# First stage of a convolution block: one reader of PSUM, squares from SBUF, padded copies two groups ahead, stores on SyncE

## The chip, the core and the metric

The kernel runs on one core of a Trainium2 chip. A core has a matrix engine (PE in the profile, with PEld for its weight loads), VectorE (DVE), ScalarE (ACT), GpSimd (POOL) and SyncE (SP), each with its own instruction queue, an on-chip memory SBUF, a smaller memory PSUM, divided into banks, into which PE writes, and DMA engines that move data to and from DRAM. An engine works through its instructions in order and waits on semaphores for what the others have to deliver. The metric is the time of one launch on the device, in microseconds (us).

## The reference

The input x has 32 images of 384 channels of 28 x 28 points, all in float32. Layer 0 is a convolution block, layer 1 a gate on its result.

```python
# layer 0
y = conv_general_dilated(x, dw_w, padding=3, feature_group_count=C)  # 7x7, each channel by itself
y = transpose(y + dw_b, (0, 2, 3, 1))
mu = mean(y, -1);  var = mean(square(y - mu), -1)
y = (y - mu) * rsqrt(var + 1e-6) * ln_g + ln_b
y = gelu(einsum('bhwc,cf->bhwf', y, w1) + b1)          # 384 -> 1536
gx = sqrt(sum(square(y), (1, 2)))
y = grn_g * (y * gx / (mean(gx, -1) + 1e-6)) + grn_b + y
x = x + transpose(einsum('bhwf,fc->bhwc', y, w2) + b2)  # 1536 -> 384
# layer 1
avg, mx, mn = mean, max, min of x over the points
logits = concat([avg @ W1.T, grouped(mx, W2_1) * W2_2, mn @ W3.T]) @ Wfc.T
return sigmoid(logits + x)
```

The part that matters here is the first: the depthwise convolution, and the mean and variance over the 384 channels, for which the kernel sums the convolved values and their squares.

## The kernel before, in words

The program has two stages. The second (from L897 on) goes image by image through the two large products, with a scheme that saves multiplications: sums and differences ("forms") of the weights and of the activations go into fewer matmuls. The first stage, the block `with ExitStack() as one`, does the depthwise convolution of all images and prepares the weight forms. The change lies in the first stage alone.

**The convolution.** The loop `for s in range(NK)` has 48 steps of 8 channels (TC). A step is four pairs of channels; `conv` handles one pair. Its input is `xt`, in which the rows of the padded image stand on the partitions and (block of rows, image) on the 224 columns. For each channel three matmuls (L696, L698, L700) multiply a band matrix of the filter (`tmat`) with `xt` into one half of a PSUM bank `pc` (pool psc, 4 banks). The bank is then read three times: DVE turns it by 32 x 32 blocks into `yt` (L703), DVE adds it to the sum `acc` (L711), and ACT squares each of the two channels into `sq` (L717, pool sqp, two tiles of half a step each). After every second pair POOL adds `sq` to `ssum` (L723). At the end of the step POOL's queue stores `yt` to `yd` in DRAM (L870). `yt` has two buffers (pool ycp). Since `keep` keeps the program order on an engine, the order in the code is the order in the queue.

**Making xt.** Four steps share one `xt`, which is made one `xt` ahead. The images come in 8 groups of 4. For each group `load_x` (SP) brings 32 channels from DRAM, 8 groups ahead. `pad_x` copies them into one of three padded tiles `xpad` (L477, on ACT; L475 on POOL for the first groups). `turn_x` then has PE turn the tile 128 x 128 at a time into a PSUM tile `pt` (L487, pool psx, 3 tiles): four blocks for h = 0, which DVE copies to `xt` (L496), and three for h = 1, which ACT copies (L498). `spread` places two groups into each step, between the pairs, and calls `pad_next(i + 1)`, so that a pad runs one group ahead of its turning.

**Loads and forms.** At the top of a step SP issues `load_t` (L424), the band matrices of three steps later. Some steps bring weights as well (`later`): before such a load a POOL copy (L816) from `acc` writes one column of its target, which holds the load back to this step. In steps 7 to 11 PE centres the first weights (`center_w`). In steps 12 to 20 and 24 to 44 `form_w` makes the weight forms u1 and u2 in three buffers (`ufp`), with an ACT or POOL instruction to start (L562, L559) and POOL additions (L565). They are stored to u1d and u2d at the end of the next step, on POOL's queue (L886).

**The end.** Steps 46 and 47 run as two halves of the images (`pc_half`), so that stage 2 can begin with the first. `finish`, once for each half, turns sums into the mean and 1/sqrt(var + eps): an add, a reduce of the four rows of `ssum` (L748), some small instructions (L754 to L757), the root on ACT (L758), a reciprocal (L759), a turn (L760) and the store to `rsd` (L761), from which stage 2 reads it back. `sq`, `ssum` and `acc` are indexed by unturned points throughout; only the result is turned.

Of the kernel before, what the change touches and what calls it, by code (L numbers as in the profile page):

```python
# [8 lines left out]
F32 = mybir.dt.float32  # L9
AF = mybir.ActivationFunctionType  # L10
# [3 lines left out]
P = 128  # L14
# [183 lines left out]
def convnext_gate_kernel(  # L198
# [163 lines left out]
    with ExitStack() as one:  # L362
# [76 lines left out]
        NG = B // NB  # L439
        NXI = 8  # L440
        xi_last = tp.tile([P, NT], F32, name="xi_last")
        ssum = finp.tile([P, SQ, N], F32, name="ssum")
        acc = finp.tile([P, 2, N], F32, name="acc")
        dws = finp.tile([P, 1], F32, name="dws")
        lr = tp.tile([P, CB, 2], F32, name="lr")
# [33 lines left out]
        def turn_x(i, h, xt, eng=nc.vector):  # L479

            g = i % NG
            xv = xt.rearrange("p c (j b) -> p j c b", j=NJ)
            j0, j1 = 4 * h, min(NJ, 4 * h + 4)
            pt = psx.tile([P, 4, P], F32, tag="pt", name=f"pt_{i}_{h}")
            for j in range(j0, j1):
                keep(
                    nc.tensor.transpose(  # L487
                        pt[:, j - j0, :],
                        xpad[i % NPAD][:, j * RW : (j + 1) * RW, :].rearrange("p r w -> p (r w)"),
                        ident,  # L490
                    )
                )
            dst = xv[:, j0:j1, :, g * NB : (g + 1) * NB]
            src = pt[:, : j1 - j0, :].rearrange("p j (c q) -> p j c q", q=NB)
            if eng is nc.vector:
                keep(eng.tensor_copy(dst, src))  # L496
            else:
                keep(eng.activation(dst, src, AF.Identity))  # L498

        def new_xt(k):  # L500
            return xtp.tile([P, XC, N], F32, tag="xt", name=f"xt_{k}")
# [114 lines left out]
        def pad_next(i):  # L616
            if i < GT:
                pad_x(i)
                if i + AHEAD < GT:
                    load_x(i + AHEAD)  # L620
# [7 lines left out]
        for i in range(NG):  # L628
# [15 lines left out]
            for h in range(2):  # L644
                turn_x(i, h, xt, (nc.vector, nc.scalar)[h])
        pad_next(NG)

        later = {
            **{
# [22 lines left out]
        def conv(s, c2, yt, xt, b0, b1):  # L672

            t = tmat[s % NT2]
            nb = b1 - b0
            if not nb:
                return
            if nb == B:
                pc = psc.tile([P, 2, 256], F32, tag="pc", name=f"pc_{s}_{c2}_{b0}")
            else:  # L680

                pc = pcs.pop(0)
                pcs.append(pc)
            for ci in range(2):
                c = 2 * c2 + ci
                if nb == B:
                    po = pc[:, ci, :N]
                    xc = xt[:, s % SK * TC + c, :]
                    after, before = xc[:, B:], xc[:, : N - B]
                    lo, hi = po[:REACH, : N - B], po[:, B:]  # L690
                else:
                    po = pc[:, ci, :N].rearrange("p (j b) -> p j b", b=B)[:, :, b0:b1]
                    xc = xt[:, s % SK * TC + c, :].rearrange("p (j b) -> p j b", b=B)[:, :, b0:b1]
                    after, before = xc[:, 1:], xc[:, : NJ - 1]
                    lo, hi = po[:REACH, : NJ - 1], po[:, 1:]
                keep(nc.tensor.matmul(po, t[:, c, P : 2 * P], xc, start=True, stop=False))  # L696
                keep(
                    nc.tensor.matmul(lo, t[:, c, 2 * P : T0 + MW], after, start=False, stop=False)  # L698
                )
                keep(nc.tensor.matmul(hi, t[:, c, :P], before, start=False, stop=True))  # L700
            cc = s * TC + 2 * c2
            cy = 2 * c2
            keep(nc.vector.transpose(yt[:, cy : cy + 2, :], pc[:, :, :N]))  # L703

            def part(v):
                if nb == B:
                    return v
                return v.rearrange("p c (j b) -> p c j b", b=B)[:, :, :, b0:b1]

            a = part(acc)  # L710
            keep(nc.vector.tensor_tensor(a, a, part(pc[:, :, :N]), ALU.add))  # L711
            nonlocal sq
            if cy % SQ == 0:
                sq = sqp.tile([P, SQ, N], F32, tag="sq", name=f"sq_{cc}_{b0}")
            for ci in range(2):
                keep(
                    nc.scalar.activation(  # L717
                        part(sq)[:, cy % SQ + ci], part(pc[:, :, :N])[:, ci], AF.Square,
                        bias=dwb[:, cc + ci : cc + ci + 1], scale=1.0,
                    )  # L720
                )
            if cy % SQ == SQ - 2:
                nc.gpsimd.tensor_tensor(part(ssum), part(ssum), part(sq), ALU.add)  # L723

        sq = None

# [2 lines left out]

        pcs = []  # L730

        fins = []

        def finish(half, b0, b1):

            if not half:
                fins.append(sqp.tile([P, SQ, N], F32, tag="sq", name="fin"))
                nc.vector.memset(fins[0][:, 0], 0.0)
            fin = fins[0]

            def part(v):
                return v.rearrange("p (j b) -> p j b", b=B)[:, :, b0:b1]

            rs, s2 = (part(fin[:, i]) for i in range(2))
            mu, va = (part(acc[:, i]) for i in range(2))
            (nc.vector.tensor_tensor(mu, mu, va, ALU.add))
            (
                nc.vector.tensor_reduce(  # L748
                    s2,
                    ssum.rearrange("p c (j b) -> p j b c", b=B)[:, :, b0:b1],  # L750
                    AX.X, ALU.add,
                )
            )
            (nc.vector.tensor_scalar(mu, mu, dws, 1.0 / C, ALU.add, ALU.mult))  # L754
            (nc.vector.tensor_tensor(va, mu, mu, ALU.mult))
            (nc.vector.scalar_tensor_tensor(va, s2, 1.0 / C, va, ALU.mult, ALU.subtract))
            (nc.vector.tensor_scalar(va, va, 0.0, EPS, ALU.max, ALU.add))  # L757
            nc.scalar.activation(s2, va, AF.Sqrt)  # L758
            (nc.vector.reciprocal(rs, s2))  # L759
            (nc.vector.transpose(fin[:, 2], fin[:, 0]))  # L760
            nc.sync.dma_start(rsd[half], fin[:, 2])  # L761

        STEPS_K = SK * PAIRS
        plan = [[] for _ in range(STEPS_K)]
# [3 lines left out]
        def spread(k, q, xn):  # L768
            for n in plan[q]:
                g, h = divmod(n, 2)  # L770
                i = k * NG + g
                if h == 0:
                    pad_next(i + 1)
                turn_x(i, h, xn, (nc.vector, nc.scalar)[h])

        def first_image(part):

# [25 lines left out]
        for s in range(NK):  # L803
# [8 lines left out]
            if s in later:  # L812

                dst, src = later[s]
                first = dst[:, :1] if len(dst.shape) == 2 else dst[:, 0, :1]
                nc.gpsimd.tensor_copy(first, acc[: dst.shape[0], 0, :1])  # L816
                nc.sync.dma_start(dst, src)
            if si == 0:
                xn = new_xt(k + 1) if k + 1 < NX else None
            if s == NK - 2:  # L820
                warm = smp.tile([P, 1], F32, tag="warm", name="warm", bufs=1)
                nc.scalar.activation(warm, eps_t, AF.Sqrt)
            if s == NK - 1:
# [33 lines left out]
            elif s < NK - 2:  # L857
                for c2 in range(PAIRS):
                    conv(s, c2, yt, xt, 0, B)
                    q = (s - U1 + 5) * PAIRS + c2  # L860
                    if 0 <= q < 2 * PAIRS:
                        for n in range(q * 3 // 2, (q + 1) * 3 // 2):
                            center_w(n)
                    elif q in (2 * PAIRS + 2, 2 * PAIRS + 5, 2 * PAIRS + 8):
                        n = FB + 4 * ((q - 2 * PAIRS) // 3)
                        for i in range(4):
                            center_w(n + i)
                    if k + 1 < NX:
                        spread(k + 1, si * PAIRS + c2, xn)
                keep(nc.gpsimd.dma_start(yd[:, s * TC : (s + 1) * TC, :], yt))  # L870
                yt = new_yt(f"yt_{s + 1}")
                if s == 35:
                    yi = yis[0] = yip.tile([P, CB, NQD, YR], F32, tag="yi", name="yi_0")
                    for cb in range(2):
                        load_y_part(0, yi, cb, 0, P)
                if NK - 4 <= s:
                    first_image(s - NK + 4)
                if s == NK - 3:
                    load_y_part(0, yis[0], CB - 1, 0, P - 2 * TC)
            if si == SK - 1:  # L880
                xt = xn
            if s == SG:
                gate_weights()
                nc.vector.tensor_reduce(dws, dwb, AX.X, ALU.add)
            for dst, u in stores:
                keep(nc.gpsimd.dma_start(dst, u))  # L886
            stores.clear()
            for i in range(NS):
                if s != U1 + i * 3 // 5:
                    continue  # L890
# [430 lines left out]
```

## Time and profile before

| | |
|---|---|
| median of 3 runs | 3113.83 us (3113.55 to 3114.8) |
| the profiled execution: its time | 3120.5 us |
| its span | 3118.8 us |
| busy in the span: PE / DVE / ACT / POOL | 97% / 64% / 58% / 80% |
| share of the last chain: PE / POOL / DMA / DVE / ACT | 79% / 7% / 5% / 4% / 2% |

The span runs from the first to the last instruction of one profiled execution. Its busy shares are averages over both stages. In the first stage, up to about 577 us, these groups matter (line, engine, operation, output and inputs, number | busy us, mean ns of one | idle before it, and what ended that):

```profile
L723 POOL TENSOR_TENSOR ssum<-ssum,sq 128x896 f32<-128x896 f32 (+1 forms) x100 | 201.2, 2012 | 142.8 <-ACT sq L717 142.3
L717 ACT ACTIVATE sq<-pc,dwb 128x224 f32<-128x224 f32 x368 | 144.2, 444 | 262.2 <-DVE acc L711 228.0 <-POOL ssum L723 24.2 <-POOL u L565 5.0
L703 DVE STREAM_TRANSPOSE yt<-pc 128x448 f32<-128x448 f32 x184 | 119.0, 647 | 225.3 <-PE pc L700 164.5 <-DMA yd<-yt 59.0 <-PE pt L487 1.6
L711 DVE TENSOR_TENSOR acc<-acc,pc 128x448 f32<-128x448 f32 x184 | 107.1, 582 | 5.5 <-POOL ws L816 5.5
L565 POOL TENSOR_TENSOR u<-u,ws 128x384 f32<-128x384 f32 (+1 forms) x66 | 68.9, 1047 | 3.4 <-ACT u L562 0.5
L477 ACT ACTIVATE xpad<-room 128x784 f32<-128x784 f32 x77 | 66.1, 858 | 0.0
L496 DVE COPY xt<-pt 128x512 f32<-128x512 f32 x96 | 65.2, 679 | 14.8 <-PE pt L487 14.7
L498 ACT ACTIVATE xt<-pt 128x384 f32<-128x384 f32 x96 | 47.0, 490 | 10.8 <-PE pt L487 7.9 <-DMA dwb<-in_cvec 3.0
L559 POOL TENSOR_TENSOR u<-ws 128x384 f32<-128x384 f32 (+1 forms) x26 | 29.1, 1126 | 44.3 <-DMA u2d<-u 27.3 <-DMA u1d<-u 12.2 <-DMA ws<-in_w 4.5
L870 POOL DMA_DIRECT2D yd<-yt x46 | 26.1, 568 | 0.0
```

The first number after the bar is the sum over all instructions of the group, the second the mean of one; the idle time that follows lies just before the instructions of the group on their engine.

### The profile page before, as it was taken

What the parts mean: (1) busy time and instruction counts of PE and PEld (TensorE: products, weight loads), DVE (VectorE), ACT (ScalarE), POOL (GpSimd) and SP (SyncE); (2) the same over time, 40 slices, a digit from 0 to 9 for tenths busy, and PEclk for the clock granted to TensorE, in tenths of its full rate; (3) what the DMA queues carried; (4) which work ended last, traced back from release to release, by engine and by line L of the source; (5) the groups of instructions that cost most, each with busy time, mean ns of one, the idle gap of its engine ahead of it and who ended that gap; (6) DMA issues with size and microseconds to landing.
All of it is one profiled execution on the core that took longest, in us unless ns stands there. A gap on an engine that the chain in (4) does not pass through costs nothing.

```text
span 3118.8 us, 44072 instructions
## 1 busy us (share of the span) xinstructions
PE 3019.9 (97%) x14435; PEld 2441.6 (78%) x14435; DVE 1992.4 (64%) x4555; ACT 1808.0 (58%) x3004; POOL 2484.5 (80%) x1912
## 2 busy tenths in 40 slices
PE   8998889799999999999999999999999999999998
PEld 8988889567777777777777777777777777777777
DVE  5554445666666666666666666666666666666666
ACT  4454445365666666666666666666666666666662
POOL 4466667569888888888888888888888888888897
PEclk9999999899999999999999999999999999999999
DMA  9888877644666666666666666666666666666545
GB/s 348 318 299 318 293 297 286 214 136 157 201 201 201 202 201 201 201 201 201 201 202 201 202 201 201 202 200 202 199 201 201 202 201 201 202 201 201 195 152 201
DMA packets 277900, 674.16 MB, mean 216 GB/s; under 512 B 30863, under 2 KB 98730, under 8 KB 271658
## 3 DMA queue, kind: packets, MB, share of 16 engines
q1 hardware_dynamic: 255364, 579.39, 56.4%
q0 software_dynamic: 9344, 53.61, 4.2%
q10 hardware_dynamic: 12966, 38.34, 3.2%
q8 instruction: 118, 1.93, 0.3%
q14 instruction: 108, 0.88, 0.1%
HBM read 575.57 MB, written 95.68 MB: 215 GB/s over the span
## 4 chain that ended last, share of the span: by engine, by line
PE 79%; POOL 7%; DMA 5%; DVE 4%; issue 2%; ACT 2%; ACTq 0%; DVEq 0%; SPq 0%; POOLq 0%
PE ph_C L974 13%; PE ph_A L974 12%; PE ph_B L974 11%; PE pz_C L1104 7%; PE pz_A L1104 7%; PE pz_D L1104 7%; PE pz_F L1104 7%; PE pc L696 2%; PE pz_H L1104 2%; PE pz_I L1104 2%; PE pz_E L1104 2%; PE pc L700 2%; PE pc L698 2%; POOL d_room L1065 2%; DVE room L315 2%
## 5 line engine op out<-in xcount | busy, mean ns | idle before, releaser
L326 ACT ACTIVATE y<-y,fv,gsc 128x784 f32<-128x784 f32 x372 | 359.1, 1031 | 463.3 <-DVE gsc L1012 463.3
L1065 POOL TENSOR_TENSOR d_room<-y 128x588 f32<-128x588 f32 x253 | 364.3, 1441 | 291.7 <-PE pz_B L1104 195.5
L933 ACT ACTIVATE y<-y,b1f 128x784 f32<-128x784 f32 x384 | 350.3, 945 | 209.8 <-DVE y L991 179.5
L974 PE MATMUL ph_C<-room,ws 128*128 128x392 f32 x1240 | 462.6, 495 | 5.8 <-DVE y L989 3.0
L974 PE MATMUL ph_B<-room,ws 128*128 128x392 f32 x1240 | 460.9, 494 | 4.2 <-DVE room L358 4.2
L974 PE MATMUL ph_A<-room,ws 128*128 128x392 f32 x1240 | 460.0, 493 | 4.0 <-ACT te L981 2.0
L1065 POOL TENSOR_TENSOR d_room<-d_room,y 128x588 f32<-128x588 f32 x308 | 440.8, 1436 | 16.8
L974 PEld LDWEIGHTS ph_C<-room,ws 128*128 128x128 f32 x1240 | 233.3, 190 | 190.1 <-DVE y L989 29.4
L974 PEld LDWEIGHTS ph_A<-room,ws 128*128 128x128 f32 x1240 | 235.7, 190 | 177.5 <-ACT te L981 2.7
L974 PEld LDWEIGHTS ph_B<-room,ws 128*128 128x128 f32 x1240 | 235.7, 191 | 169.4 <-POOL ssum L723 4.3
L946 ACT ACTIVATE junk<-y 128x784 f32<-128x784 f32 x384 | 329.0, 857 | 9.0
L1065 POOL TENSOR_TENSOR d_room<-y,d_room 128x588 f32<-128x588 f32 x214 | 306.1, 1436 | 26.9 <-PE pz_D L1104 15.8
L723 POOL TENSOR_TENSOR ssum<-ssum,sq 128x896 f32<-128x896 f32 (+1 forms) x100 | 201.2, 2012 | 142.8 <-ACT sq L717 142.3
L358 POOL TENSOR_TENSOR room<-room 128x392 f32<-128x392 f32 x303 | 303.5, 1019 | 11.9
L717 ACT ACTIVATE sq<-pc,dwb 128x224 f32<-128x224 f32 x368 | 144.2, 444 | 262.2 <-DVE acc L711 228.0
L1065 POOL TENSOR_TENSOR y<-y 128x588 f32<-128x588 f32 x180 | 258.7, 1437 | 7.1
L703 DVE STREAM_TRANSPOSE yt<-pc 128x448 f32<-128x448 f32 x184 | 119.0, 647 | 225.3 <-PE pc L700 164.5
L987 DVE TENSOR_TENSOR y<-y,ph_B 128x392 f32<-128x392 f32 x256 | 137.4, 557 | 156.0 <-ACT y L933 123.5
L985 DVE TENSOR_TENSOR y<-y,ph_C 128x392 f32<-128x392 f32 x384 | 212.5, 560 | 25.2
L696 PE MATMUL pc<-xt,tmat 128*128 128x224 f32 x736 | 205.9, 362 | 8.9 <-ACT xt L498 8.9
L1104 PE MATMUL pz_A<-d_room,u 128*128 128x196 f32 x1050 | 202.8, 329 | 0.1
L1104 PEld LDWEIGHTS pz_A<-d_room,u 128*128 128x128 f32 x1050 | 178.9, 190 | 7.4 <-POOL d_room L1065 0.4
(267 smaller groups left out, 6434.1 us busy)
## 6 DMA issues: line engine op xcount, KB each, us to landing
u<-u2d SPq DMA_DIRECT2D x487, 384.0 KB, 3.8
ws<-u1d SPq DMA_DIRECT2D x384, 320.0 KB, 3.0
tmat<-fs SPq DMA_DIRECT2D x47, 1420.0 KB, 8.6
ws<-u2d SPq DMA_DIRECT2D x121, 384.0 KB, 3.7
yi<-yd SPq DMA_DIRECT2D x95, 448.0 KB, 6.5
yd<-yt POOLq DMA_DIRECT2D x46, 896.0 KB, 6.8
x<-in_x SPq DMA_DIRECT2D x32, 1176.0 KB, 5.6
out<-x ACTq DMA_DIRECT2D x31, 1176.0 KB, 9.9
```

What stands on the lines that cost most here:

```text
L326: eng.activation(out, in_, AF.Identity, bias=add, scale=mul)
L358: tc.keep_in_program_order(eng.tensor_tensor(d, o[in0], o[in1], op))
L696: keep(nc.tensor.matmul(po, t[:, c, P : 2 * P], xc, start=True, stop=False))
L717: nc.scalar.activation(part(sq)[:, cy % SQ + ci], part(pc[:, :, :N])[:, ci], AF.Square, bias=dwb[:, cc + ci : cc + ci + 1], scale=1.0,)
L723: nc.gpsimd.tensor_tensor(part(ssum), part(ssum), part(sq), ALU.add)
L933: ins = nc.scalar.activation(y, y, AF.Gelu, bias=b1f[:, f : f + 1], scale=1.0)
L946: ins = nc.scalar.activation(junk, ys[b][:, f, :], AF.Square, accum_out=ssqs[b][:, f : f + 1])
L974: nc.tensor.matmul(banks[t, bk][:, :NH], wts[t][:, i % UG, :], o[opnd], start=(first == 1), stop=True, skip_group_check=True,)
L985: nc.vector.tensor_tensor(d, d, p, ALU.add)
L987: nc.vector.tensor_tensor(d, d, p, ALU.subtract)
L1065: nc.gpsimd.tensor_tensor(d[0], o[a][0], o[c][0], ALU.add if sign == "+" else ALU.subtract)
L1104: nc.tensor.matmul(pz[:, :NQ4], wt[:, i % UD, t, :], o[opnd][0][:, t, :], start=(first and t == 0), stop=(t == KD - 1), skip_group_check=True,
```

## The change

- ACT squares the turned values, `yt` in SBUF, instead of the bank `pc`. The squares and `ssum` are therefore indexed by turned points, and `finish` turns the sum of `acc` first and works on turned points after that.
- All copies of `pt` to `xt` in the loop are made by DVE (those of the first `xt` still alternate between DVE and ACT).
- `pad_next` runs two groups ahead instead of one, with three `xpad` tiles as before.
- `yd` is stored by SP. The weight forms are stored by SP too, in the middle of the step after the one that makes them.
- The POOL copies that held back the `later` loads are gone; SP issues the loads in program order.
- In the halves the squares and `ssum` cover whole rows of points of both channels. The first half's sum of squares goes to a tile `s2` of its own, whose first addition takes `ssum` as base and leaves `ssum` as it is for the second half.
- The temporaries of `finish` and `s2` are slices of one more `xt` buffer, made at step 46.

```diff
-        ssum = finp.tile([P, SQ, N], F32, name="ssum")
+        ssum = finp.tile([P, SQ, YR], F32, name="ssum")
...
         pad_next(NG)
+        pad_next(NG + 1)
...
-                sq = sqp.tile([P, SQ, N], F32, tag="sq", name=f"sq_{cc}_{b0}")
+                sq = sqp.tile([P, SQ, YR], F32, tag="sq", name=f"sq_{cc}_{b0}")
             for ci in range(2):
                 keep(
                     nc.scalar.activation(
-                        part(sq)[:, cy % SQ + ci], part(pc[:, :, :N])[:, ci], AF.Square,
+                        sq[:, cy % SQ + ci], yt[:, cy + ci], AF.Square,
                         bias=dwb[:, cc + ci : cc + ci + 1], scale=1.0,
                     )
                 )
             if cy % SQ == SQ - 2:
-                nc.gpsimd.tensor_tensor(part(ssum), part(ssum), part(sq), ALU.add)
+                to, base = ssum, ssum
+                if nb < B and not b0:
+                    to = late["s2"]
+                    base = ssum if s == NK - 2 and cy < SQ else to
+                nc.gpsimd.tensor_tensor(to, base, sq, ALU.add)
...
+            mu0, s1, mu, va, s2, rs = (late[f"t{6 * half + i}"] for i in range(6))
+            nc.vector.tensor_tensor(part(mu0), part(acc[:, 0]), part(acc[:, 1]), ALU.add)
+            nc.vector.transpose(s1, mu0)
+            nc.vector.tensor_reduce(
+                s2, (ssum if half else late["s2"]).rearrange("p c n -> p n c"), AX.X, ALU.add
             )
...
             nc.scalar.activation(s2, va, AF.Sqrt)
-            (nc.vector.reciprocal(rs, s2))
-            (nc.vector.transpose(fin[:, 2], fin[:, 0]))
-            nc.sync.dma_start(rsd[half], fin[:, 2])
+            nc.vector.reciprocal(rs, s2)
+            nc.sync.dma_start(rsd[half], rs)
+
+        def late_tiles():
+
+            t = new_xt(NX).rearrange("p c n -> p (c n)")
+            late["s2"] = t[:, : SQ * YR].rearrange("p (c n) -> p c n", n=YR)
+            for i in range(12):
+                late[f"t{i}"] = t[:, (SQ + i) * YR : (SQ + i + 1) * YR]
+            for half in range(2):
+                nc.gpsimd.memset(late[f"t{6 * half}"], 0.0)
...
                 if h == 0:
-                    pad_next(i + 1)
-                turn_x(i, h, xn, (nc.vector, nc.scalar)[h])
+                    pad_next(i + 2)
+                turn_x(i, h, xn)
...
                 dst, src = later[s]
-                first = dst[:, :1] if len(dst.shape) == 2 else dst[:, 0, :1]
-                nc.gpsimd.tensor_copy(first, acc[: dst.shape[0], 0, :1])
-                nc.sync.dma_start(dst, src)
+                keep(nc.sync.dma_start(dst, src))
...
             if s == NK - 2:
+                late_tiles()
...
                     conv(s, c2, yt, xt, 0, B)
+                    if c2 == PAIRS // 2:
+                        for dst, u in stores:
+                            keep(nc.sync.dma_start(dst, u))
+                        stores.clear()
...
-                keep(nc.gpsimd.dma_start(yd[:, s * TC : (s + 1) * TC, :], yt))
+                keep(nc.sync.dma_start(yd[:, s * TC : (s + 1) * TC, :], yt))
...
-            for dst, u in stores:
-                keep(nc.gpsimd.dma_start(dst, u))
-            stores.clear()
```

More of the change, by code (lines that the diff above doesn't have):

```diff
@@ L730, in convnext_gate_kernel @@
         pcs = []
-        fins = []
+        late = {}
         def finish(half, b0, b1):
[L736 to L739, printed above, removed]
             def part(v):
                 return v.rearrange("p (j b) -> p j b", b=B)[:, :, b0:b1]
[L744 to L752, printed above, removed]
-            )
[L754 to L757, printed above, removed]
+            mu0, s1, mu, va, s2, rs = (late[f"t{6 * half + i}"] for i in range(6))
[3 more added lines that the diff above has]
+                s2, (ssum if half else late["s2"]).rearrange("p c n -> p n c"), AX.X, ALU.add
+            )
+            nc.vector.tensor_scalar(mu, s1, dws, 1.0 / C, ALU.add, ALU.mult)
+            nc.vector.tensor_tensor(va, mu, mu, ALU.mult)
+            nc.vector.scalar_tensor_tensor(va, s2, 1.0 / C, va, ALU.mult, ALU.subtract)
+            nc.vector.tensor_scalar(va, va, 0.0, EPS, ALU.max, ALU.add)
```

## The prediction

> **What bounds the kernel now.** I read the slices first, then the windows, the waits and the timeline. In the page's forty slices of 78 us PE's digit is 9 from slice 9 on; only the first eight, 620 us, have room, and the change touches just these.
>
> ```profile
> PE   8998889799999999999999999999999999999998
> PEclk9999999899999999999999999999999999999999
> ```
>
> The windows put a number on it (columns: stretch, length, then PE, PEld, DVE, ACT and POOL busy with instruction counts, PE clock, DMA share, GB/s):
>
> ```profile
> 23.10:92.10 69.00, 68.86 (x432) 66.05 (x431) 40.89 (x73) 37.58 (x83) 31.43 (x25) 0.99 1.02 375
> 255.50:275.40 19.90, 10.28 (x62) 9.46 (x62) 6.05 (x14) 5.62 (x14) 15.92 (x15) 0.87 0.66 226
> 458.00:527.50 69.50, 68.99 (x434) 66.21 (x433) 40.76 (x72) 41.53 (x94) 57.55 (x49) 1.00 0.82 303
> 527.50:544.50 17.00, 17.00 (x107) 16.61 (x106) 9.45 (x20) 8.74 (x20) 10.64 (x10) 1.00 0.77 279
> 544.50:577.00 32.50, 21.22 (x181) 20.73 (x179) 16.19 (x39) 9.75 (x33) 18.88 (x18) 0.84 0.56 179
> ```
>
> Rows one and three are seven conv steps each in which PE never stops: 69.5 / 7 = 9.93 us a step. Row two is one step that took 19.9 with PE busy for 10.3: a stall. Row four is steps 44 and 45, row five the two image halves of steps 46 and 47. So PE is the floor and stalls lie on it. What they wait for, up to 620 us (engine, line, releaser: total us, times, longest):
>
> ```profile
> ACT sq L717 <- DVE acc L711: 245.0, 159, 13.1
> DVE yt L703 <- PE pc L700: 164.5, 143, 8.3
> POOL ssum L723 <- ACT sq L717: 142.3, 64, 10.6
> DVE yt L703 <- DMA yd<-yt: 59.0, 14, 8.3
> PE pt L487 <- ACT xpad L477: 36.9, 10, 9.6
> ACT sq L717 <- POOL ssum L723: 27.3, 8, 5.6
> POOL u L559 <- DMA u2d<-u: 27.3, 5, 8.0
> POOL u L559 <- DMA u1d<-u: 12.2, 4, 4.9
> DVE yt_a L703 <- DMA yd<-yt: 12.2, 1, 12.2
> PE pc_half L696 <- ACT sq L717: 9.8, 2, 8.3
> DVE acc L711 <- POOL ws L816: 5.5, 1, 5.5
> ```
>
> PE itself waits for few things, mostly pads; the ring behind them is what to see. A POOL form (L559) waits for the store of its buffer, or a yt for its store, which POOL issues; ssum on POOL is late; squares (L717) wait; the pad behind them on ACT is late; PE's turning of that pad stops. The timeline of ACT in that 19.9 us step (start, length, operation, idle before in brackets) shows it: nothing from 258 to 272, then a square, with the pad behind it.
>
> ```profile
> 258.24 0.88 ACT L477 ACTIVATE xpad<-room 128x784 f32<-128x784 f32 x1
> 272.21 0.79 ACT L717 ACTIVATE sq<-pc,dwb 128x224 f32<-128x224 f32 x2 [13.09 <-DVE acc L711]
> ```
>
> **What the skill says.** "PSUM — Partial Sum Buffer", section on PSUM bank collisions: two engines must not touch one bank at once, reads by ScalarE and VectorE included. The trace agrees in its effect: a square waits for acc, another reader of the bank, 159 times. "TensorE: Matmul & The Clock Gate", section What's actually happening: an idle window of about 3.4 us drops the clock to half; the stalled window has 0.87, the full ones 0.99 and 1.00, so a removed stall gives a little more than its idle time. "DMA: Bandwidth & Descriptors", section Issuing engines are not separate DMA queues: the same 16 engines serve all issuers; moving an issue saves only issuing time. The same page's Specifications give an HBM limit of about 358 GB/s per core, which is exceeded here (375 for 69 us with PE full); the measurement decides.
>
> **The sum available.** Steps 0 to 43 at 9.93 are 437; steps 44 and 45 take 17; weight centring in steps 7 to 11 is PE work of about 8 (my estimate from steps 8, 9 and 10 lasting 12.3, 12.0 and 11.4). That is 462 against the 521.4 between 23.1 and 544.5: 59 us. In the halves PE is busy 21.2 of the 31 us up to its last conv matmul at 575.5: 10 us. All stalls gone would give 69.
>
> **Part by part.**
> *Squares from yt.* ACT then waits for the transpose alone; acc alone frees the bank. The 245 us in which ACT waits for acc cost nothing by themselves, but they hold pads. A square from PSUM lasts 444 ns; SBUF has no row of this form. A pad from SBUF is 858 ns for 784 columns, an ACT copy from PSUM 490 for 384: near in slope, so I take 444, bounds 400 to 510. At eight a step the upper bound is +0.5 us on an ACT with half its time free. New: yt is reused after its squares as well as its store; squares trail the transpose by a pair or so, yt by a step.
> *Copies L498 to DVE.* ACT loses 47.0 us in all, two of 0.49 a step. DVE gains 128x384 copies: its row shows 679 ns for 512 columns, so between 0.51 (pure slope) and 0.60; I take 0.55. DVE per step is 4 x (0.65 + 0.58) + 2 x 0.68 + 2 x 0.55 = 7.4 of 9.93 us: hidden, 75% full. ACT falls to about 8 x 0.44 + 2 x 0.86 = 5.2.
> *Pads two groups ahead.* Two groups per step, so slack for a pad rises from 5 to 10 us. POOL and yt stalls reached 8.0 and 8.3; nearly all fit, the ring in the first 44 steps opens.
> *Stores to SP, holds gone.* POOL loses 46 issues of 0.57 (26.1 us), 34 of u (21.7) and its hold copies, one of which held acc 5.5 us. POOL then has 2 x 2.08 of ssum and (68.9 + 29.1) / 34 = 2.9 of forms a step, 7.1; in the fullest window 57.55 / 7 = 8.2: it fits. On SP each step issues load_t, a later load, x loads, u store (mid-step), yd store. In the instruction order of the changed kernel as built, each u store's form is issued on POOL before the middle of its step, and what stands behind it, the yd store and the next load_t, has two to three steps of lead. Bounds: nothing to 2.5 us a step, I take nothing. The gate's wait for its weights (10.3 once, on DVE) gets two steps more and goes.
> *DMA at the faster pace.* Per step tmat 1.45 MB, yd 0.92, x 0.80: 3.17, plus (15 x 256 + 19 x 384 KB) / 34 = 0.34 of u: 3.5 MB in 9.93 us, 354 GB/s, under the 375 sustained. Bounds: 0 to 20 us in all.
> *Halves.* Squares and ssum now run over whole rows: a pair's squares near 0.79 for 0.60, ssum 2.08 eight times, 16.6 us beside 21 of PE: hidden. The yd wait of 12.2 before yt_a comes from POOL issuing step 45's store behind forms; on SP it is issued at once, and some 2 us remain while it lands.
> *End of stage.* The late tiles use an xt buffer, and stage 2's first y lies over it: the built order has ACT's first eviction (L981 now, L985 then) wait for both rsd stores and both reciprocals. Reciprocal goes from 0.85 to about 1.7 and the reduce from about 0.85 to 1.35, twice each. Before, that ACT eviction came 6 us after the last acc (576.9) and the fourth group of matmuls at 586.5, 9.6 after; the last reciprocal ended 10.1 after; with 0.85 more in each of two reciprocals and 0.5 in each reduce, less the two turns of 0.4 that go, some 12.2; 0.5 to the issue and 1.7 to land (as rsd did) make 14.4, the fourth group comes at about 15: +5.4. Part returns, since POOL's 21.9 us wait for d_room<-rsd ends some 5 earlier and later PE waits on it shrink. Bounds 0 to +6; I take +2.
> *What stays late.* Yd store in the halves 2, the w2 load before its form (4.5 before) 2, a tenth of the 44 us of form waits, 4: 8.
>
> Sum: 69 - 8 - 2 = 59, about 60 with the clock's share. The profiled execution goes from 3120.5 (span 3118.8) to 3060.5; the median, 6.7 below it, from 3113.8 to 3054.
>
> **Rivals.**
> (a) A new floor in the middle. DMA holds 340 instead of 375 GB/s (3.5 MB: 10.3 us), or DVE, alone emptying PSUM at 75%, delays pt and pc to 10.5. Over 46 steps 0.4 is 18 us, 0.57 is 26: 3072 to 3080. For it: row one stands at DMA share 1.02. Against: PE was full there.
> (b) The ring stays: pads still stand behind squares on ACT, and squares still wait for ssum (27.3 us before) and ssum for forms. If a stall is seldom under 10 us, two groups don't cover it; a third of the gain is left, about 24 us: 3090. Against: the longest store wait is 8.3.
> (c) Slower: SP, in order, stands at a u store until POOL's form is done, and yd's store and the loads behind it wait; yt and tmat then stop DVE and PE. It decides from 60 / 34 = 1.8 us per step with forms; at 2.5 it costs 85 and gives 3139. For it: POOL is the fullest engine there but PE. Against: the half step given to the form.
> (d) Gains and losses cancel: 3114.
>
> **How the numbers follow.** Forecast 0.58 (alone 3045 to 3064: no residue and no tail at the low end, tail and residue doubled at the high end), (a) 0.22, (b) 0.10, (c) 0.08, (d) 0.02. Faster is the first three, 0.90. The range must reach over (a): 3044 to 3086 leaves out (b), (c), (d) and slivers, just under 2 in 10 with the lower part of (b) counted. A measurement here can't tell less than 0.2%, 6 us, from nothing.
>
> **What would show it.** Right: steps near 9.9 us from 23 us to the halves; ACT's squares waiting for the transpose and no longer for acc; PE's waits for pads near zero; DVE near 7.4 us a step; halves near 22 us; ACT's first eviction later after the last acc than 6 us. Wrong: PE waiting for DVE copies or tmat in even steps of 10.3 and more (a), for pads in single long stops (b), SP's stores waiting for POOL (c), or conv's end near 510 with the total unmoved, the tail then being far dearer than +2.

## The result, and the profile after

| | before | changed |
|---|---|---|
| median, same chip (4 runs each) | 3114.32 us (3113.55 to 3116.74) | 3061.15 us (3059.55 to 3062.09) |
| ratio, 95% interval | | 0.9827 [0.981, 0.9844] |
| the profiled execution, its span | 3120.5, 3118.8 us | 3060.9, 3059.1 us |

The change saves 53 us by the medians and 60 by the profiled executions, since the profiled one of before was 6 us slower than its median. The windows of the changed kernel's profile, cut at the same events as those of before (columns as there), are steps 0 to 6, steps 7 to 45, the two halves up to the last conv matmul, and the passage into stage 2:

```profile
23.77:99.05 75.28, 69.92 (x432) 67.13 (x431) 46.78 (x87) 34.27 (x69) 27.14 (x13) 0.95 0.98 357
99.05:487.23 388.18, 388.18 (x2490) 377.48 (x2489) 269.05 (x482) 199.54 (x412) 257.21 (x173) 1.00 0.93 346
487.23:507.21 19.98, 19.61 (x186) 19.28 (x184) 15.51 (x36) 11.45 (x29) 19.43 (x12) 1.00 0.93 290
507.21:526.60 19.39, 7.70 (x12) 3.23 (x12) 15.51 (x25) 4.20 (x11) 4.57 (x3) 0.70 0.73 202
```

In the second row PE is busy for all of its 388 us at full clock: 39 steps without a stall. Before, the same steps took 452.4 us with PE busy for 408.3:

```profile
92.10:544.50 452.40, 408.34 (x2495) 390.01 (x2494) 232.78 (x407) 216.29 (x487) 296.21 (x246) 0.95 0.82 299
```

So 44.1 of the 64.2 us that went were idle time of PE, and 20.1 were time in which the same matmuls ran slower: the granted clock was 0.95 before and is 1.00, and 388.2 is 0.95 of 408.3. The other rows of the changed kernel are less clean. Set side by side with the profile before:

| stretch | before | changed | difference |
|---|---|---|---|
| steps 0 to 6 | 69.0 | 75.3 | +6.3 |
| steps 7 to 45 | 452.4 | 388.2 | -64.2 |
| halves, to the last conv matmul | 31.0 | 20.0 | -11.0 |
| last conv matmul to the last matmul of stage 2 | 2532.9 | 2541.3 | +8.5 |

The last row counts to the start of that matmul. With 0.7 us more ahead of step 0 these make the 59.7 us by which the spans differ. So two losses of 15 us together stand against a gain of 75. The waits of the changed kernel up to 560 us show what went and what came:

```profile
ACT sq L718 <- DVE yt L704: 223.6, 170, 9.0
...
DVE yt L704 <- DMA yd<-yt: 20.8, 6, 8.6
...
ACT y L985 <- DMA rsd<-xt: 8.0, 1, 8.0
...
PE ph_B L978 <- issue: 6.1, 1, 6.1
...
PE pt L487 <- DVE xt L496: 4.9, 1, 4.9
...
DVE yt_a L704 <- DMA yd<-yt: 3.5, 1, 3.5
```

The wait of the transpose for the store of yt fell from 59.0 us to 20.8, and 16.5 of these lie in steps 2 to 4. PE's wait for ACT's pads (36.9) and the forms' waits for their stores (39.5) are gone from the list. New is the third line, at the passage to stage 2.

### The profile page after: what moved, and what is told of

It reads as the page before. It is cut to its first block, busy times and chain, and to the rows that moved or that the text cites. A ratio compares the mean times of both kernels' runs of the same rounds, so it can differ in the third digit from the quotient of the medians.

```text
span 3059.1 us, 43987 instructions
## 1 busy us (share of the span) xinstructions
PE 3000.1 (98%) x14435; PEld 2428.2 (79%) x14435; DVE 2038.2 (67%) x4642; ACT 1792.1 (59%) x2916; POOL 2445.7 (80%) x1822
## 4 chain that ended last, share of the span: by engine, by line
PE 87%; POOL 4%; DVE 4%; DMA 2%; ACT 1%; issue 1%; DVEq 0%; ACTq 0%; SPq 0%; POOLq 0%
PE ph_C L978 13%; PE ph_A L978 12%; PE ph_B L978 11%; PE pz_A L1108 8%; PE pz_C L1108 8%; PE pz_F L1108 7%; PE pz_D L1108 7%; PE pc L697 4%; PE pc L699 4%; PE pc L701 4%; PE pt L487 2%; PE pz_H L1108 2%; PE pz_I L1108 2%; PE pz_E L1108 2%; POOL d_room L1069 2%; DVE room L315 2%
## 5 line engine op out<-in xcount | busy, mean ns | idle before, releaser
L728 POOL TENSOR_TENSOR ssum<-ssum,sq 128x896 f32<-128x896 f32 x96 | 200.7, 2090 | 176.6 <-ACT sq L718 175.2
L358 POOL TENSOR_TENSOR room<-room 128x392 f32<-128x392 f32 x303 | 303.5, 1018 | 11.9
L718 ACT ACTIVATE sq<-yt,dwb 128x224 f32<-128x224 f32 x376 | 160.5, 474 | 233.6 <-DVE yt L704 223.6
```

The costliest lines, as they stand in the source:

```text
L358: tc.keep_in_program_order(eng.tensor_tensor(d, o[in0], o[in1], op))
L718: nc.scalar.activation(sq[:, cy % SQ + ci], yt[:, cy + ci], AF.Square, bias=dwb[:, cc + ci : cc + ci + 1], scale=1.0,)
L728: nc.gpsimd.tensor_tensor(to, base, sq, ALU.add)
```

## The experiments

Each kernel ran on one chip with the kernel before beside it. The chips differ by a few us (medians of before 3108 to 3114), so a kernel is compared by its ratio to before on its chip, or by its trace. On one chip the kernel before spread from 3103.4 to 3121.7 us over 29 runs; the changed kernel's four runs lie within 2.6. The interval of a ratio is thus 3 to 9 us wide to each side or so, and differences below that among the fast versions are read from the traces, not from the ratios.

**What the losses are: the end of stage 1.**

```diff
-            for i in range(12):
-                late[f"t{i}"] = t[:, (SQ + i) * YR : (SQ + i + 1) * YR]
-            for half in range(2):
-                nc.gpsimd.memset(late[f"t{6 * half}"], 0.0)
+            for half in range(2):
+                u = ufp.tile([P, UD * KD, P], F32, tag="uf", name=f"fin_{half}")
+                u = u.rearrange("p c n -> p (c n)")
+                for i in range(3):
+                    late[f"t{3 * half + i}"] = u[:, i * YR : (i + 1) * YR]
+                nc.gpsimd.memset(late[f"t{3 * half}"], 0.0)
```

In `finish`, three tiles for each half then do for six (mu overwrites s1; va and rs overwrite mu0).

> As the changed kernel, but finish() keeps its temporaries in two weight-form buffers instead of the extra xt buffer, so stage 2's first y no longer lies over them. If ACT's wait for the rsd stores sets the end of stage 1 (8.0 us in the changed kernel), the fourth group of matmuls comes 6 to 8 us sooner after the last conv matmul and the time falls from 3061 to 3053 to 3055. If the later first matmul (6.1 us after the conv instead of 4.2, DVE busy with the first image) sets it, the gain is under 2 us: 3059 to 3061.

Measured: 3053.9 us, ratio 0.9814 [0.9791, 0.9836]. The timeline of ACT (start, length, idle before in brackets), first of the changed kernel, then of this one:

```profile
517.68 0.39 ACT L754 ACTIVATE xt<-xt 128x224 f32<-128x224 f32 x1 [3.30 <-DVE xt L753]
526.05 0.89 ACT L985 ACTIVATE y<-ph_B 128x392 f32<-128x392 f32 x2 [7.98 <-DMA rsd<-xt]
```

```profile
517.71 0.39 ACT L755 ACTIVATE fin<-fin 128x224 f32<-128x224 f32 x1 [3.37 <-DVE fin L754]
518.00 0.86 ACT L988 ACTIVATE y<-ph_B 128x392 f32<-128x392 f32 x2
```

The last root ends at the same time in both; the eviction then follows at once instead of 8 us later. The fourth group of matmuls comes 15.3 us after the conv instead of 19.4, and the last matmul of stage 2 comes 2534.4 after it instead of 2541.3: 6.9 us back. The first theory holds, with the time in its range, though the group itself came 4.1 us sooner and not 6 to 8. All fourteen traces agree on this stretch: the six with the finish of before have 2528.8 to 2533.3 us from the last conv matmul to the last one of stage 2, the six with the new finish in the extra `xt` buffer 2539.9 to 2543.3, the two with its tiles moved 2534.4 and 2535.2. The 1.5 us left against the 2532.9 of before are about what the first matmul is late, 6.2 us after the conv instead of 4.2.

**What the losses are: the first steps.**

```diff
-                keep(nc.sync.dma_start(yd[:, s * TC : (s + 1) * TC, :], yt))
+                st = nc.gpsimd if s < 6 else nc.sync
+                keep(st.dma_start(yd[:, s * TC : (s + 1) * TC, :], yt))
```

> As the changed kernel, but yd of steps 0 to 5 is stored from POOL's queue again. If SP's order makes the stall in steps 0 to 6 (x loads that wait for pads stand ahead of the yd store, yd ahead of the transpose, the transpose ahead of the squares and pads), these seven steps take 69 us again instead of 75.3 and the time is about 3055. If the transfers themselves are late there (DMA full), moving the issue changes nothing: 3059 to 3062.

Measured: 3055.5 us (3053.1 to 3060.4), ratio 0.9825 [0.9796, 0.9853]. The ratio alone doesn't tell it from the changed kernel's 0.9827; the trace does. Its span is 3051.2, 7.9 below the changed kernel's. Steps 0 to 6 took 67.4 us with PE busy for all of them, at 379 GB/s, so the transfers had not been the limit. What had, can be read in SP's timeline of the changed kernel:

```profile
38.92 11.92 SPq L458 DMA_DIRECT2D room<-in_x  x2
50.93 0.54 SPq L877 DMA_DIRECT2D yd<-yt  x1
...
53.37 9.85 SPq L458 DMA_DIRECT2D xi_last<-in_x  x1
63.31 0.56 SPq L458 DMA_DIRECT2D room<-in_x  x1
63.96 0.54 SPq L877 DMA_DIRECT2D yd<-yt  x1
```

Step 2 ends at 53.0 (its last transpose), and its yd store is issued at 63.96, behind x loads. These wait on ACT's pads (SP waited 162.6 us for L477 in all, most of it harmless), and a pad waits behind squares, squares wait for a transpose, and that transpose waits for a buffer whose store is this one or the one before it. The ring that the change opened at POOL closes at SP. In DVE's timeline of the changed kernel it costs 8.6 us in step 4:

```profile
71.91 0.65 DVE L704 STREAM_TRANSPOSE yt<-pc 128x448 f32<-128x448 f32 x1 [8.62 <-DMA yd<-yt]
```

With the repair, steps 7 and 8 give 2 us back (14.4 and 13.1 us, for 11.9 and 13.6): there DVE waits 8.4 us for the gate's weights, a wait that is not in the changed kernel's list.

**Which part gains: undoing one at a time.** One group of pad slack instead of two:

```diff
-        pad_next(NG + 1)
...
-                    pad_next(i + 2)
+                    pad_next(i + 1)
```

> As the changed kernel, but pads one group ahead, as before. If the second group of slack is what hides the stalls, PE waits for pads again and the time rises by 15 to 40 us, to 3076 to 3100. If the stalls went because ACT's squares and POOL are no longer late, nothing needs the slack: 3060 to 3064, PE's wait for pads under 3 us.

Measured: 3062.1 us, ratio 0.9839 [0.9816, 0.9862]. No stall came back in the steps: 7 to 45 take 388.2 us, as in the changed kernel. The halves take 22.9 us for 20.0, but so they do (23.1) in the run below with the copies on ACT, which keeps the pads two groups ahead. The rival holds.

Squares from PSUM (and, in `finish`, a transpose of the reduced sum of squares):

```diff
-                        sq[:, cy % SQ + ci], yt[:, cy + ci], AF.Square,
+                        sq[:, cy % SQ + ci], pc[:, ci, :N], AF.Square,
```

> As the changed kernel, but ACT squares from the PSUM bank again (and finish turns the sum of squares). If sharing the bank was the cause of the stalls, they come back: 3080 to 3100. If the bank only ordered the three readers, and the slack of pads and the free POOL carry the gain: 3060 to 3066, since four banks cover the extra reader.

Measured: 3064.4 us, ratio 0.9848 [0.9825, 0.9871]; the conv ends 3.0 us later than in the changed kernel (510.2 for 507.2), nearly all of it by step 4 and in the halves. A third reader of the bank decides next to nothing.

The stores back on POOL:

```diff
-                    if c2 == PAIRS // 2:
-                        for dst, u in stores:
-                            keep(nc.sync.dma_start(dst, u))
-                        stores.clear()
...
-                keep(nc.sync.dma_start(yd[:, s * TC : (s + 1) * TC, :], yt))
+                keep(nc.gpsimd.dma_start(yd[:, s * TC : (s + 1) * TC, :], yt))
...
+            for dst, u in stores:
+                keep(nc.gpsimd.dma_start(dst, u))
+            stores.clear()
```

> As the changed kernel, but yd and the weight forms are stored from POOL's queue again (forms at the end of the step). If POOL's stores, with a store behind forms and a form behind a store, made the stalls, most of them come back: 3080 to 3105, with waits of the transpose for yd<-yt. If the two groups of pad slack and the squares from SBUF absorb POOL's lateness, or these were the cause: 3060 to 3068; a fall to 3055 is included, since the start gains 6 us as in the run with yd of the first steps on POOL.

Measured: 3113.3 us, ratio 1.0006 [0.9997, 1.0016]. With everything else of the change in place, nothing is gained in all. (Where the rest acts can be guessed from single traces only: the conv ends at 557.4, for 563.4 in the run with the pads alone below, and the new finish takes this back, so that the spans are 3107.7 and 3107.1 us.) The waits say why (this kernel, up to 620 us):

```profile
DVE yt L704 <- DMA yd<-yt: 89.7, 18, 11.9
...
POOL u L559 <- DMA u2d<-u: 17.3, 6, 3.8
POOL u L559 <- DMA u1d<-u: 16.2, 4, 5.1
```

and POOL's timeline shows how the two belong together:

```profile
240.16 2.07 POOL L728 TENSOR_TENSOR ssum<-ssum,sq 128x896 f32<-128x896 f32 x1
247.36 1.31 POOL L559 TENSOR_TENSOR u<-ws 128x512 f32<-128x512 f32 x1 [5.13 <-DMA u1d<-u]
248.75 3.97 POOL L565 TENSOR_TENSOR u<-u,ws 128x512 f32<-128x512 f32 x3
253.01 0.77 POOL L889 DMA_DIRECT2D u1d<-u  x1 [0.29 <-POOL u L565]
253.80 2.09 POOL L728 TENSOR_TENSOR ssum<-ssum,sq 128x896 f32<-128x896 f32 x1
255.83 0.57 POOL L873 DMA_DIRECT2D yd<-yt  x1
```

A form waits 5.1 us for the store of its buffer; the yd store of the step that ended at 239.1 is behind it in the queue and goes out at 255.8, 16.7 us late. In a step without forms it goes out 3.1 us after the step's last transpose, behind the last ssum, and lands 8 to 13 us after that transpose; the one that needs the buffer comes about 11 us after it (a step of 9.8 and the next pair's matmuls). There is hardly any slack, and two groups of pads do nothing for a transpose.

The copies back on ACT:

```diff
-                turn_x(i, h, xn)
+                turn_x(i, h, xn, (nc.vector, nc.scalar)[h])
```

> As the changed kernel, but the 128x384 copies of the turned tiles are done by ACT again. If they cost what the sums say (ACT at 5.2 + 1.0 us of 9.9 a step), nothing: 3060 to 3064. If ACT's queue was the narrow place, in that a copy stood between squares and pads, stalls return: 3070 to 3090.

Measured: 3059.3 us, ratio 0.9833 [0.9816, 0.9851]: nothing, as the sums had it.

**Which part gains: one alone, on the kernel before.** Both kinds of stores on SP, in the middle of the next step and at the end of the step:

```diff
+                    if c2 == PAIRS // 2:
+                        for dst, u in stores:
+                            keep(nc.sync.dma_start(dst, u))
+                        stores.clear()
...
-                keep(nc.gpsimd.dma_start(yd[:, s * TC : (s + 1) * TC, :], yt))
+                keep(nc.sync.dma_start(yd[:, s * TC : (s + 1) * TC, :], yt))
...
-            for dst, u in stores:
-                keep(nc.gpsimd.dma_start(dst, u))
-            stores.clear()
```

> As the kernel before, with the one difference that SP stores yd and the weight forms (forms in the middle of the step). If POOL's stores made the stalls, most of the gain comes from this alone: 3055 to 3075. If the shared bank or the pads' slack is needed too, it stays above 3090; if SP's waits at the stores are a cost of their own, it may be above 3112.

Measured: 3056.8 us, ratio 0.9826 [0.981, 0.9842]. This is as much as the whole change gains, from its stores alone; the POOL copies that hold back the loads are still there. The course differs: the conv ends at 513.7, 6.5 us later than in the changed kernel, and the finish of before more than makes up for it. Nor is SP's way to DRAM the faster one. The pages before and after give, as the last number, the median from issue to landing:

```profile
yd<-yt POOLq DMA_DIRECT2D x46, 896.0 KB, 6.8
yd<-yt SPq DMA_DIRECT2D x47, 896.0 KB, 6.6
```

So it is the time of issue that changed. ACT still waits 209 us for acc and PE's weight loads 12 us for pads, and neither stops PE for long: steps 7 to 45 take 393.3 us with PE busy for 391.9. The waits of this run, up to 620 us:

```profile
PEld pt L487 <- ACT xpad L477: 12.3, 21, 4.9
...
DVE yt L703 <- DMA yd<-yt: 10.9, 3, 5.5
```

Pads two groups ahead alone:

```diff
+        pad_next(NG + 1)
...
-                    pad_next(i + 1)
+                    pad_next(i + 2)
```

> As the kernel before, with the one difference that pads run two groups ahead. If slack alone covers POOL's lateness: 3065 to 3090. If pads two groups ahead still stand behind the same squares on ACT: 3105 to 3116, as before.

Measured: 3108.7 us, ratio 0.9995 [0.9987, 1.0004]: no change. Yet the pads did get their slack: PE's wait for ACT's pads (36.9 us before) is no longer in the list. In its place the transpose waits longer for the stores, 97.6 us where it was 59.0 (up to 620 us):

```profile
DVE yt L704 <- DMA yd<-yt: 97.6, 20, 8.7
```

The stall has moved, not gone.

Each kind of store alone: first `yd` (the second hunk of the stores' diff), then the weight forms (its first and third):

> As the kernel before, with yd alone stored by SP; the weight forms stay on POOL's queue. If yd's store, issued on POOL behind forms that wait for their buffers, makes the stalls: close to the run with both stores on SP, 3055 to 3068. If the forms' own stores on POOL (a form waits for its buffer, ssum and squares behind it) make them: above 3090.

> As the kernel before, with the weight forms alone stored by SP, in the middle of the step; yd stays on POOL's queue. If yd's store on POOL makes the stalls: 3090 to 3112, the transpose still waiting 40 us or more for yd<-yt. If the forms' stores make them: 3055 to 3070.

Measured: 3096.1 us, 0.9961 [0.9946, 0.9975], and 3091.4 us, 0.9947 [0.9931, 0.9964]. The first lies in the range for "the forms' stores", the second in the range for "yd's store", so neither is the cause by itself: yd alone gives 12 us, the forms alone 17, both together 54. With yd on SP these waits stay (up to 620 us)

```profile
ACT sq L717 <- POOL ssum L723: 54.6, 12, 7.9
POOL u L559 <- DMA u2d<-u: 32.7, 8, 10.5
...
PE pt L487 <- ACT xpad L477: 23.3, 7, 6.4
```

and with the forms on SP these:

```profile
DVE yt L703 <- DMA yd<-yt: 36.1, 10, 10.7
...
PE pt L487 <- ACT xpad L477: 13.4, 9, 4.1
...
DVE yt_a L703 <- DMA yd<-yt: 12.0, 1, 12.0
```

In the first, forms still wait for their buffers, and ssum, squares and pads behind them: the ring as I had read it before. In the second the forms on POOL wait for their stores for only 11.3 us in all (7.0 for u2d, 4.3 for u1d; 39.5 before), but POOL reaches the yd store late behind forms and ssum (up to 13.0 us after the step's last transpose, 3.5 at best), and the transpose waits. There are two causes in one queue, and in many steps each hides the other.

**Versions that beat both kernels.** The first is the changed kernel with both repairs (the first two diffs above); the second is the kernel before with both stores on SP (yd of steps 0 to 5 from POOL), the copies on DVE and the pads two groups ahead, its squares and `finish` untouched:

```diff
+        pad_next(NG + 1)
...
-                    pad_next(i + 1)
-                turn_x(i, h, xn, (nc.vector, nc.scalar)[h])
+                    pad_next(i + 2)
+                turn_x(i, h, xn)
...
+                    if c2 == PAIRS // 2:
+                        for dst, u in stores:
+                            keep(nc.sync.dma_start(dst, u))
+                        stores.clear()
...
-                keep(nc.gpsimd.dma_start(yd[:, s * TC : (s + 1) * TC, :], yt))
+                st = nc.gpsimd if s < 6 else nc.sync
+                keep(st.dma_start(yd[:, s * TC : (s + 1) * TC, :], yt))
...
-            for dst, u in stores:
-                keep(nc.gpsimd.dma_start(dst, u))
-            stores.clear()
```

> The changed kernel with both repairs: temporaries of finish in weight-form buffers, yd of steps 0 to 5 from POOL. Alone they gave 7.2 and 5.7 us; in different places, they should add: 3047 to 3050. If one hides in the other: 3053 to 3055.

> The kernel before, with its squares from PSUM and its finish, and these parts of the change: stores on SP (yd of steps 0 to 5 from POOL), all copies on DVE, pads two groups ahead. If the squares from SBUF are not needed and the old end of stage 1 is the shorter one: conv's end near 504, the time 3043 to 3049. If the squares from PSUM bring stalls back in this order: 3055 or more.

Measured on one chip: 3051.4 us, 0.9819 [0.9805, 0.9834], and 3047.0 us, 0.9805 [0.979, 0.982]. The repairs add for the most part in the spans (3046.2, 12.9 below the changed kernel's, for 7.2 and 7.9 singly); the median of the first lies between its two forecasts. The second is the fastest of all, with a span of 3045.8 and four runs within 1 us, all below the four of the first, and does without the squares from SBUF and the new end of the stage. By ratio alone neither interval is clear of the changed kernel's.

## Why the prediction was right, and where it was not

- **What bounds it, and the sum available.** Right. Stalls lay on a PE floor; from step 7 to 45 all of them went. The floor was set at 9.93 us a step and is 9.77 (four steps of 39.06), because small waits of 0.3 us in two steps of four went as well; either the pads or the copies suffice for that, as the runs without one of them keep it, while stores alone on the kernel before don't (39.6 for four). The conv ends 68.3 us earlier, where I took 69 less 8. That a removed stall gives "a little more than its idle time" was too small: 20.1 us on top of 44.1. It didn't spoil the sum, which for these steps was a difference of lengths and so held the slower matmuls already.
- **Pads two groups ahead: "the ring in the first 44 steps opens".** Wrong, and the step that failed. I gave this part the gain. Alone it changes nothing (0.9995), and taken out it costs next to nothing (3062.1). The argument from the longest store wait, 8.3 us, against 10 us of slack looked only at the pads; the transpose waits for a yd store directly, and no pad stands in that path (97.6 us of such waits with the pads alone).
- **Stores to SP, holds gone.** I counted POOL's issuing time, 48 us of an engine with time to spare, and so nothing. It was the whole gain (0.9826 alone, with the holds kept). What counts is not how long an issue takes but when an in-order engine reaches it: yd goes out 0.0 to 2.7 us after the step's last transpose in nearly all steps after the fifth, where POOL took 3.5 at best and up to 18.0 before. The Trainium skill's "DMA: Bandwidth & Descriptors", section Issuing engines are not separate DMA queues, from which I took that only issuing time is saved, speaks of the initiation itself; these runs show that the queue of work ahead of it can be worth 54 us.
- **Squares from yt.** Each lasts 474 ns, within the bounds (444 taken). That it freed the pads is not borne out: 3 us.
- **Copies to DVE.** 543 ns each, as taken (0.55); DVE 47.3 us in seven steps, 6.8 a step for 7.4. Nothing gained or lost.
- **DMA.** No limit: 346 GB/s over steps 7 to 45, 379 in the repaired first seven. Rival (a) is out.
- **SP "nothing".** Right from step 7 on; in the first steps SP's order cost 6.3 us. It is rival (c)'s kind, in that yd stands behind a waiting instruction, but the wait is that of the x loads for pads, not that of a form.
- **Halves.** 11 us gained, 10 less 2 expected; the wait before yt_a is 3.5, where 2 was taken.
- **End of stage.** The mechanism was right, the term too small: +8.5 for +2. The fourth group of matmuls comes 17.7 us after the last acc (19.4 after the conv), for 15 estimated. DVE's last reciprocal ends 14.0 us after the last acc, for 12.2: the terms as given add to 12.0, and they take off two turns that don't go but only move ahead of the reduce; the reduce lasts 1.67 us for 1.35; and two instructions are held up (last section). The rsd store is issued straight after it and holds ACT for 3.1 us, for 0.5 to the issue and 1.7 to land. The part that was to return from d_room didn't: POOL's first work after the conv waits, by the profile, for PE's ph_B (31.2 us) and not for rsd, and 8.3 us are still missing 600 matmuls later.
- **The median.** The profiled executions differ by 59.6 us, the forecast was 60. The 6.7 us by which the profiled run of before lay over its median were carried over as if they belonged to profiling. In the changed kernel the profiled run and the median agree (3060.9 and 3061.15), so they belonged to that one run; that is the 7 us between 3054 and 3061. That its stalls vary from run to run is likely, but not shown: versions almost without stalls spread by about 7 us too (3053.1 to 3060.4 with yd of the first steps on POOL).

So the size came out nearly right for a wrong share-out: the available sum was read from PE's idle time, which doesn't say which part of a change will free it, and 15 us of losses, for 2 forecast at the end of the stage, met 75 us of gain, for 69 less 8. That these two errors cancelled in the profiled pair was luck.

## What to carry to other kernels

An engine with time to spare can still issue a DMA too late: for each store ask what stands ahead of it in its in-order queue and what that waits for, and compare the time from the last write to the landing with the time until the buffer is needed again. Slack given to another link of the ring can just move the stall. Where two causes sit in one queue, undo both before judging either: here they gave 12 and 17 us alone and 54 together. After moving an issue, look for the new instruction that waits ahead of it, and at what later memory lies over a temporary that a store still reads.

## What the runs showed of the hardware

At the end of stage 1 some DVE instructions last several times their usual time. The timeline of DVE in the changed kernel, then that of POOL:

```profile
508.81 1.50 DVE L751 TENSOR_TENSOR xt<-xt 128x224 f32<-128x224 f32 x1
510.23 2.22 DVE L790 TENSOR_SCALAR room<-yi,cv 128x392 f32<-128x392 f32 x1
...
514.93 0.39 DVE L751 TENSOR_TENSOR xt<-xt 128x224 f32<-128x224 f32 x1
```

```profile
507.98 4.25 POOL L728 TENSOR_TENSOR ssum<-ssum,sq 128x896 f32<-128x896 f32 x2 [0.38 <-ACT sq L718]
```

The same multiplication takes 1.50 us while POOL adds and 0.39 when it doesn't; the tensor_scalar takes 2.22, for 0.41 in the kernel before, and ends within 0.3 us of POOL's second addition (512.2). In the run with one group of pad slack the order is another, and the roles change: the multiplication meets the addition and takes 2.25, the tensor_scalar comes after it and takes 0.38. DVE and POOL there:

```profile
512.90 2.25 DVE L750 TENSOR_TENSOR xt<-xt 128x224 f32<-128x224 f32 x1
515.41 0.38 DVE L789 TENSOR_SCALAR room<-yi,cv 128x392 f32<-128x392 f32 x1
```

```profile
510.58 4.33 POOL L727 TENSOR_TENSOR ssum<-ssum,sq 128x896 f32<-128x896 f32 x2 [1.23 <-ACT sq L717]
```

The Trainium skill, "GPSIMD Engine Reference", section Key points, names such a contention: the two engines share their way to SBUF where a DVE instruction has two SBUF inputs or runs in a two-port mode. The traces agree with that for the multiplication; the tensor_scalar has one tensor input, and its mode was not tried. Together the two lose 2.9 us in the changed kernel. That this is why stage 2's first matmul is 1.9 us late fits in size, but no run was made to show it.
